# Transposing the softmax weights by 32 x 32 squares and DMA in place of TensorE, in a fused attention and experts kernel

## The chip, the cores and the metric

The kernel runs on one core of a Trainium2 chip. The metric is the device time of one execution in microseconds (us), as a median over runs. The core has five engines, each of which runs its own instructions in order: TensorE (PE in the profile, with PEld for its weight loads), VectorE (DVE), ScalarE (ACT), GpSimd (POOL) and SyncE (SP). Engines wait for each other through semaphores. SP and ACT issue plain DMAs, GpSimd issues indirect ones, and sixteen DMA engines carry the packets of all of them.

## What is computed

Eight images of 256 channels and 32 x 32 places go through two layers, all in float32. Layer 0 is an attention with eight heads, whose softmax runs over the queries. Layer 1 takes the 1024 places of an image as tokens `t` of 256 numbers:

```python
t = t + _L1_attn_ref(_ln_t(t), L1_attn_W)
t = t + _L1_ffn_ref(_ln_t(t), router_w, w1, b1, w2, b2)   # 8 experts, best 2 of each token

def _L1_attn_ref(x, W):
    xa = jnp.einsum('bnd,ed->bne', x, W)
    scores = jnp.einsum('bne,bme->bnm', xa, x)
    attn = jax.nn.softmax(scores, axis=-1)
    return jnp.einsum('bnm,bmd->bnd', attn, x)
```

The change lies in the last line: the product of the 1024 x 1024 weights `attn` with the normed tokens.

## The kernel before

The kernel is written in a tile language: a scheduler orders each engine's instructions and sets the semaphores, and tiles with the same tag share a fixed number of buffers. Images are handled one after the other. For each image `b` the kernel runs `layer0`, then `attend` (the first line above), then the routing of the tokens to experts. For images 0 to 6 the routed tokens are scattered to DRAM, and the experts run once for all seven after layer 0 of image 7. Image 7 runs `attend` while results of the other seven are collected, and then its experts densely.

`attend` treats the 1024 tokens in eight blocks of 128 (`NT` = 8, `P` = 128). It norms the tokens into `n1`, turns them to channels (`nT`), and multiplies by `W` (`xa`). Then, for block `i`:

- `scores(i)`: four matmuls (L670) write the block's 128 x 1024 scores to PSUM (`ps1`, one of three buffers of the tag "big"). VectorE takes the maximum of each row (L678). ScalarE writes the exponentials `ex` to SBUF and their sums `ssum` (L681). `ex` is in a pool of six buffers with the tag "exps", each 128 x 1024.
- `mix(i)`: a matmul that sums over the tokens `m` needs `m` on the partitions, and `ex` has them along its rows. So TensorE transposes eight 128 x 128 pieces against an identity (L689), VectorE copies the 128 x 1024 result from PSUM to `aT` in SBUF (L691), and eight matmuls with `aT` as the stationary side add up `py` (L695). VectorE scales by the reciprocal of `ssum` and adds the tokens (L699, L701).

The loop at L706 issues `mix` one block behind `scores`. TensorE's order that comes of it is: the transposes of block i, half of the scores of block i + 2, the products of block i, the other half of those scores. While VectorE and ScalarE work, TensorE also does products of the next image (`fill`, `pv` and `pqk`, L387 and L328). SP loads the next image (`xT`, L93) and its 32 x 32 squares (`xs`, L427, eight DMAs of 128 KB in runs of 512 bytes).

Two operations elsewhere in the kernel resemble what the change adds. The stores of the results (L1186, L1193) transpose a 128 x 1024 tile on VectorE by 32 x 32 squares and send it off in DMAs of 256 runs of 512 bytes; the last four of them are issued by ACT. `b_v` (L118) is loaded in 1024 runs of 256 bytes.

The functions before the change, with the profile's line numbers:

Of the kernel before, what the change touches and what calls it, by code (L numbers as in the profile page):

```python
# [10 lines left out]
F32 = mybir.dt.float32  # L11
# [8 lines left out]
def kernel(  # L20
# [23 lines left out]
    nc = tc.nc  # L44
    P = 128
    B, C, S = x.shape
    E, D, FF = w1.shape
# [4 lines left out]
    NT = S // P  # L52
# [15 lines left out]
    expp = ctx.enter_context(tc.tile_pool(name="expp", bufs=6))  # L68
# [6 lines left out]
    def big(name):  # L75

        return ps_big.tile([P, 1024], F32, tag="big", name=name)

    def acc(name):

        return ps_acc.tile([P, 512], F32, tag="acc", name=name)
# [54 lines left out]
    for e in range(E):  # L136
# [30 lines left out]
        fill=0.0,  # L167
# [42 lines left out]
    SQ = 32  # L210
    NQ = P // SQ
# [40 lines left out]
    def layer_norm(t, dst, eps, name):  # L252
        return Norm(t, dst, eps, name).blocks(0, NT)

    def to_channels(t, dst, name):

        for cc in range(NCC):
            pt = big(f"pt_{name}_{cc}")
            for i in range(NT):
                nc.tensor.transpose(pt[:, ts(i, P)], t[:, i, ts(cc, P)], ident)  # L260
            copied = nc.vector.tensor_copy(dst[:, cc, :], pt)
        return copied
# [380 lines left out]
    def attend(b, t1, fill, tick=nothing):  # L643
        n1 = one.tile([P, NT, D], F32, tag="n", name=f"n1_{b}")
        layer_norm(t1, n1, 1e-5, f"a{b}")
        fill("norm 1")
        nT = one.tile([P, NCC, S], F32, tag="nT", name=f"nT_{b}")
        to_channels(n1, nT, f"n1_{b}")
        fill("normed 1")
        xa = one.tile([P, NCC, S], F32, tag="xa", name=f"xa_{b}")  # L650
        for ec in range(NCC):
            px = big(f"px_{b}_{ec}")
            for dc in range(NCC):
                for n in range(NH2):
                    nc.tensor.matmul(  # L655
                        px[:, ts(n, 512)],
                        WT[:, dc, ts(ec, P)],
                        nT[:, dc, ts(n, 512)],
                        start=(dc == 0),
                        stop=(dc == NCC - 1),  # L660
                    )
            tick(("xa", ec), nc.vector.tensor_copy(xa[:, ec, :], px))

        t2 = t1

        def scores(i):
            psc = big(f"ps1_{b}_{i}")
            for ec in range(NCC):
                for n in range(NH2):
                    nc.tensor.matmul(  # L670
                        psc[:, ts(n, 512)],
                        xa[:, ec, ts(i, P)],
                        nT[:, ec, ts(n, 512)],
                        start=(ec == 0),
                        stop=(ec == NCC - 1),
                    )
            nmax = small.tile([P, 1], F32, tag="nmax", name=f"nmax_{b}_{i}")
            tick(("max", i), nc.vector.tensor_reduce(nmax, psc, AX.X, ALU.max, negate=True))  # L678
            ex = expp.tile([P, 1024], F32, tag="exps", name=f"ex1_{b}_{i}")
            ssum = small.tile([P, 1], F32, tag="ssum", name=f"ssum_{b}_{i}")  # L680
            nc.scalar.activation(ex, psc, AF.Exp, bias=nmax, scale=1.0, accum_out=ssum)  # L681
            return ex, ssum

        def mix(i, ex, ssum):
            if i == NT - 1:
                fill("last weights")
            pt = big(f"pa_{b}_{i}")
            for m in range(NT):
                nc.tensor.transpose(pt[:, ts(m, P)], ex[:, ts(m, P)], ident)  # L689
            aT = two.tile([P, S], F32, tag="tr", name=f"aT_{b}_{i}")  # L690
            nc.vector.tensor_copy(aT, pt)  # L691
            ahead = fill("last products") if i == NT - 1 else None
            py = acc(f"py_{b}_{i}")
            for m in range(NT):
                nc.tensor.matmul(  # L695
                    py[:, :D], aT[:, ts(m, P)], n1[:, m, :], start=(m == 0), stop=(m == NT - 1)
                )
            rs = small.tile([P, 1], F32, tag="rs1", name=f"rs1_{b}_{i}")
            nc.vector.reciprocal(rs, ssum)  # L699
            with tc.issue_after(ahead.ins) if ahead else nullcontext():  # L700
                mixed = nc.vector.scalar_tensor_tensor(  # L701
                    t2[:, i, :], py[:, :D], rs, t1[:, i, :], ALU.mult, ALU.add
                )
            tick(("mixed", i), mixed)

        pending = None  # L706
        for i in range(NT):
            now = (i, *scores(i))
            if pending is not None:
                mix(*pending)  # L710
            pending = now
        mix(*pending)
        return t2


# [87 lines left out]
    def normed(b, t2, fill, tick=nothing, norm=None):  # L803

        if norm is None:
            n2 = one.tile([P, NT, D], F32, tag="n", name=f"n2_{b}")
            tick("normed", layer_norm(t2, n2, 1e-5, f"f{b}"))
        else:
            n2 = norm.dst
            tick("normed", norm.blocks(NT - 1, NT))  # L810
        fill("norm 2")
        nT = one.tile([P, NCC, S], F32, tag="nT", name=f"n2T_{b}")
        tick("turned", to_channels(n2, nT, f"n2_{b}"))

        nc.gpsimd.tensor_add(t2, t2, n2)  # L815
        fill("normed 2")
        l = logits(b, nT)
        return n2, nT, l
# [256 lines left out]
    class Results:  # L1075
# [94 lines left out]
        def tick(self, place, behind=None):  # L1170
            added, sent, stored = self.PLACES.get(place, (0, 0, 0))
            if added:
                with tc.issue_after(behind.ins):
                    for _ in range(added):
                        self.add()
            for _ in range(sent):
                self.gather(behind)
            for _ in range(stored):
                if self.whole:
                    b, total, n = self.whole.pop(0)  # L1180
                    store(b, total, n)
# [130 lines left out]
    for b in range(B):  # L1312
        xT = next_x
        if b + 1 < B:
            next_x = load_x(b + 1)
        if b > 0:
            xs = load_squares(b)
        t1 = layer0(b, xT, begun, routing, xs)
        if b + 1 < B:
            begun = Begin(b + 1, next_x)  # L1320
            t2 = attend(b, t1, begun.at)
            n2, _, l = normed(b, t2, begun.at)
            nc.sync.dma_start(groups[0].sums[b], t2)
            routing = dispatch(b, n2, l, groups[0])
            continue
        experts(groups[0])
        others = Results(groups[0])
        others.begin()
        norm = None

        def fill(place):

            nonlocal norm
            others.tick(place)
            if place == "last products":
                norm = Norm(t1, one.tile([P, NT, D], F32, tag="xa", name=f"n2_{b}"), 1e-5, f"f{b}")
                return norm.blocks(0, NT - 1)

        t2 = attend(b, t1, fill, others.tick)
        dense(b, t2, norm, others.tick)  # L1340
        assert others.added == len(others.units) and not others.whole
# [42 lines left out]
```

## Time and profile before

| | us |
|---|---|
| median of 3 runs | 2407.27 |
| lowest and highest | 2404.34 to 2408.37 |
| profiled execution, its own time | 2406.31 |
| its span, first to last instruction | 2404.6 |
| TensorE busy in it | 2359.7 |
| VectorE busy | 1540.9 |
| ScalarE busy | 938.0 |
| `attend` of the second image, scores(0) to the last product | 66.95 |

The profile is one execution of the program. In a group of instructions the last column says how long the engine had been idle before them and who ended that; the column before it gives the total busy time and the mean duration of one. The chain of waits is followed back from the last instruction to what released it each time; what lies on it sets the time.

### The profile page before, as it was taken

The numbers are of one execution on the slowest core, as the hardware profiler recorded it, in microseconds if no ns is written. First come the engines' busy times: TensorE is split into PE (matmuls) and PEld (weight loads), VectorE is DVE, ScalarE is ACT, GpSimd is POOL, SyncE is SP. The second block draws the span as 40 slices with busy tenths as digits, with TensorE's granted clock in tenths as the row PEclk, the third lists the DMA queues.
The fourth block names the chain that finished last, engine by engine and source line by source line (L and its number), as shares of the span: only waits on it lengthen the run. The fifth ranks groups of instructions, "written<-read, shape, count | busy, mean of one in ns | idle before, by whom it ended". The sixth has DMA issues, their size and how long they took to land.

```text
span 2404.6 us, 36813 instructions
## 1 busy us (share of the span) xinstructions
PE 2359.7 (98%) x13759; PEld 1316.5 (55%) x13759; DVE 1540.9 (64%) x3660; ACT 938.0 (39%) x1570; POOL 420.0 (17%) x391
## 2 busy tenths in 40 slices
PE   9999999999999999999999999999999999999898
PEld 3356534654466336633664356435653388887565
DVE  5775587457845785578647864687468753334776
ACT  3651366126611662156315641465136622221111
POOL 0000012000200020003000200020002234444563
PEclk9999999999999999999999999999999999999899
DMA  8993201010101010001000100100010256665454
GB/s 294 386 386 101 53 19 36 1 36 12 43 1 35 8 47 1 18 18 54 1 18 18 47 8 6 31 25 12 1 36 19 74 176 220 219 219 161 142 170 119
DMA packets 114778, 196.59 MB, mean 82 GB/s; under 512 B 15752, under 2 KB 58408, under 8 KB 112808
## 3 DMA queue, kind: packets, MB, share of 16 engines
q1 hardware_dynamic: 88504, 126.52, 15.8%
q0 software_dynamic: 25008, 67.20, 9.1%
q8 instruction: 109, 1.79, 0.3%
q10 hardware_dynamic: 1088, 0.52, 0.1%
q14 instruction: 69, 0.57, 0.1%
HBM read 108.88 MB, written 110.90 MB: 91 GB/s over the span
## 4 chain that ended last, share of the span: by engine, by line
PE 91%; DVE 5%; ACT 2%; DMA 1%; issue 1%; POOL 0%; SPq 0%; DVEq 0%; ACTq 0%; POOLq 0%
PE po L545 19%; PE psc L468 18%; PE py L695 9%; PE ps L670 7%; PE pqk L350 7%; PE pr L636 5%; PE ph L1021 4%; PE pv L387 4%; PE pe L1046 4%; PE pdh L1250 2%; PE px L655 2%; PE pdy L1274 2%; PE pa L689 2%; PE pqk L328 2%; PE px L1011 1%
## 5 line engine op out<-in xcount | busy, mean ns | idle before, releaser
L509 ACT ACTIVATE ex<-psc,nmax 128x1024 f32<-128x1024 f32 x512 | 570.5, 1115 | 312.6 <-DVE scrap L492 227.8
L468 PE MATMUL psc<-qk,qk 64*64 64x512 f32 x4096 | 578.4, 594 | 10.3 <-ACT ex L509 10.3
L545 PE MATMUL po<-ex,vs 64*64 64x512 f32 x4096 | 573.5, 592 | 1.3 <-DVE vs L525 0.3
L492 DVE TENSOR_SCALAR_CACHE_REDUCE scrap<-psc,nmax 128x512 f32<-128x512 f32 x512 | 384.4, 751 | 152.0 <-PE psc L468 126.2
L483 DVE TENSOR_REDUCE nmax<-psc 128x1 f32<-128x512 f32 x512 | 350.3, 684 | 9.3 <-PE psc L468 9.3
L468 PEld LDWEIGHTS psc<-qk,qk 64*64 64x64 f32 x4096 | 181.0, 132 | 285.8 <-ACT ex L509 138.0
L545 PEld LDWEIGHTS po<-ex,vs 64*64 64x64 f32 x4096 | 177.9, 132 | 273.5 <-issue 81.7
L695 PE MATMUL py<-n,aT 128*128 128x256 f32 x1024 | 238.0, 386 | 2.9 <-DVE aT L691 2.9
L670 PE MATMUL ps<-nT,xa 128*128 128x512 f32 x512 | 236.0, 592 | 0.0
L695 PEld LDWEIGHTS py<-n,aT 128*128 128x128 f32 x1024 | 191.7, 191 | 66.6 <-DVE aT L691 41.8
L884 POOL DMA_INDIRECT rows<-n,d_at x112 | 108.8, 972 | 662.6 <-DVE nmax L483 662.3
L681 ACT ACTIVATE ex<-ps,nmax 128x1024 f32<-128x1024 f32 x64 | 71.3, 1115 | 348.0 <-DVE nmax L678 333.5
L815 POOL TENSOR_TENSOR t<-t,n 128x2048 f32<-128x2048 f32 x8 | 36.3, 4534 | 924.0 <-DVE n L242 924.0
L350 PE MATMUL pqk<-xT,wqkv 128*128 128x512 f32 x384 | 171.2, 599 | 0.0
L701 DVE SCALAR_TENSOR_TENSOR t<-py,rs,t 128x256 f32<-128x256 f32 x64 | 30.9, 482 | 194.4 <-PE py L695 194.4
L670 PEld LDWEIGHTS ps<-nT,xa 128*128 128x128 f32 x512 | 93.5, 190 | 81.2 <-issue 75.1
L350 PEld LDWEIGHTS pqk<-xT,wqkv 128*128 128x128 f32 x384 | 71.0, 190 | 99.9 <-issue 77.8
L1130 POOL DMA_INDIRECT yk<-y,yat x112 | 110.6, 988 | 72.4 <-issue 26.8
L636 PEld LDWEIGHTS pr<-wo,res 128*128 128x128 f32 x512 | 120.7, 331 | 3.7 <-ACT res L563 3.7
L636 PE MATMUL pr<-wo,res 128*128 128x256 f32 x512 | 121.6, 398 | 0.3 <-ACT res L563 0.3
L387 PE MATMUL pv<-wqkv,xT 128*128 128x512 f32 x256 | 120.3, 599 | 1.4 <-DVE v L395 1.0
L315 ACT ACTIVATE qk<-pqk,b_qks 128x512 f32<-128x512 f32 x124 | 85.6, 691 | 88.9 <-PE pqk L350 79.8
(189 smaller groups left out, 2479.8 us busy)
## 6 DMA issues: line engine op xcount, KB each, us to landing
rows<-wb SPq DMA_DIRECT2D x7, 8192.0 KB, 51.7
y<-yb SPq DMA_DIRECT2D x63, 256.0 KB, 2.4
xs<-in_x_dram SPq DMA_DIRECT2D x64, 128.0 KB, 3.9
out_dram<-oT SPq DMA_DIRECT2D x60, 128.0 KB, 2.9
xT<-in_x_dram SPq DMA_DIRECT2D x7, 1024.0 KB, 5.0
sums<-t SPq DMA_DIRECT2D x7, 1024.0 KB, 3.9
o<-sums SPq DMA_DIRECT2D x7, 1024.0 KB
wpack<-in_L_ffn_w_dram SPq DMA_DIRECT2D x4, 1024.0 KB
```

The costliest lines, as they stand in the source:

```text
L350: mm = nc.tensor.matmul(pq[:, ts(n, 512)], wqkv[:, cc, t, ts(g, P)], xT[:, cc, ts(n, 512)], start=(cc == 0), stop=(cc == NCC - 1),)
L387: nc.tensor.matmul(pv, self.xT[:, cc, ts(i, P)], wqkv[:, cc, 2, :], start=(cc == 0), stop=(cc == NCC - 1),)
L468: mm = nc.tensor.matmul(pss[at, h][ts(c, DK), ts(n, 512)], k[r, j * P + c * DK : j * P + (c + 1) * DK], q[r, ts(n, 512)], start=True, stop ...
L483: firsts[at, h] = nc.vector.tensor_reduce(nmax, pss[at, h][:, ts(0, 512)], AX.X, ALU.max, negate=True)
L492: seconds[h] = nc.vector.tensor_scalar(scrap, pss[at, h][:, ts(1, 512)], -1.0, nmaxes[at, h], ALU.mult, ALU.min, accum_out=nmax,)
L509: nc.scalar.activation(ex, pss.pop((at, h)), AF.Exp, bias=nmaxes.pop((at, h)), scale=1.0, accum_out=sums[at][:, h : h + 1],)
L545: mm = nc.tensor.matmul(po[n][ts(h, DK), :], vss[at][keys, h, :], exps[at, h][keys, ts(n, 512)], start=(j == 0 and turn == 0), stop=(j == ...
L636: nc.tensor.matmul(pr[:, :C], own(res[:, g, :], i), wo[:, g, :], start=(g == 0), stop=(g == NPAIR - 1))
L670: nc.tensor.matmul(psc[:, ts(n, 512)], xa[:, ec, ts(i, P)], nT[:, ec, ts(n, 512)], start=(ec == 0), stop=(ec == NCC - 1),)
L695: nc.tensor.matmul(py[:, :D], aT[:, ts(m, P)], n1[:, m, :], start=(m == 0), stop=(m == NT - 1))
L884: scatter = nc.gpsimd.indirect_dma_start(out=view[:, :], out_offset=bass.IndirectOffsetOnAxis(ap=ats[k][:, i : i + 1], axis=0), in_=n2[:, ...
L1130: ins = nc.gpsimd.indirect_dma_start(out=self.slot(at)[:, k, :], out_offset=None, in_=self.group.y[:, :], in_offset=bass.IndirectOffsetOnAxis(
```

## The change

For blocks 0 to 6 the weights are no longer transposed on TensorE. VectorE transposes each 32 x 32 square of `ex` in place (`sq`). Sixteen DMAs, eight from SP and eight from ACT, then move the squares to where they belong in a dense `aT`: DMA (a, k) reads the 32 partitions of group a and writes the 32 partitions of group k, in 256 runs of 32 numbers (128 bytes), 32 KB in all. `sq` and `aT` are taken from the six "exps" buffers. Block 7 is turned as before. `mix` now runs two blocks behind the scores in the program's text instead of one, and the last two turned blocks and block 7 are mixed after the loop.

```diff
-        def mix(i, ex, ssum):
-            if i == NT - 1:
-                fill("last weights")
+        def turn(i, ex):
+            sq = expp.tile([P, S], F32, tag="exps", name=f"sq_{b}_{i}")
+            nc.vector.transpose(sq, ex)
+            aT = expp.tile([P, S], F32, tag="exps", name=f"aT_{b}_{i}")
+            to = aT.rearrange("p (m a q) -> p a m q", a=NQ, q=SQ)
+            since = sq.rearrange("p (m k q) -> p k m q", k=NQ, q=SQ)
+            for a in range(NQ):
+                queue = (nc.sync, nc.scalar)[a % 2]
+                for k in range(NQ):
+                    queue.dma_start(to[ts(k, SQ), a], since[ts(a, SQ), k])
+            return [aT[:, ts(m, P)] for m in range(NT)]
+
+        def turn_last(i, ex):
             pt = big(f"pa_{b}_{i}")
             for m in range(NT):
                 nc.tensor.transpose(pt[:, ts(m, P)], ex[:, ts(m, P)], ident)
             aT = two.tile([P, S], F32, tag="tr", name=f"aT_{b}_{i}")
             nc.vector.tensor_copy(aT, pt)
+            return [aT[:, ts(m, P)] for m in range(NT)]
+
+        def mix(i, aT, ssum):
             ahead = fill("last products") if i == NT - 1 else None
             py = acc(f"py_{b}_{i}")
             for m in range(NT):
                 nc.tensor.matmul(
-                    py[:, :D], aT[:, ts(m, P)], n1[:, m, :], start=(m == 0), stop=(m == NT - 1)
+                    py[:, :D], aT[m], n1[:, m, :], start=(m == 0), stop=(m == NT - 1)
                 )
...
-        pending = None
+        pending = []
         for i in range(NT):
-            now = (i, *scores(i))
-            if pending is not None:
-                mix(*pending)
-            pending = now
-        mix(*pending)
+            ex, ssum = scores(i)
+            if i < NT - 1:
+                pending.append((i, turn(i, ex), ssum))
+            if i > 1:
+                mix(*pending.pop(0))
+        fill("last weights")
+        pending.append((NT - 1, turn_last(NT - 1, ex), ssum))
+        for some in pending:
+            mix(*some)
```

Here `SQ` is 32 and `NQ` is 4. In the changed file the transpose on VectorE stands at L688, the DMAs at L695, the products at L711 and the update at L717.

## The prediction

> **What bounds the kernel now.** I read the page first: busy shares and the chain that ended last.
>
> ```profile
> PE 2359.7 (98%) x13759; PEld 1316.5 (55%) x13759; DVE 1540.9 (64%) x3660; ACT 938.0 (39%) x1570; POOL 420.0 (17%) x391
> PE 91%; DVE 5%; ACT 2%; DMA 1%; issue 1%; POOL 0%; SPq 0%; DVEq 0%; ACTq 0%; POOLq 0%
> ```
>
> TensorE (PE) carries 91% of the chain, so work taken off it shortens the kernel wherever nothing else becomes late. Next the chain of waits in the second image's `attend` (449.31 to 516.26 us, 66.95 us), which holds all that the change touches:
>
> ```profile
> 449.31 3.45 PE ps L670 x8
> ...
> 456.64 1.09 PE pa L689 x8
> 457.73 1.72 PE ps L670 x4
> 459.45 3.45 PE py L695 x16
> 462.90 1.72 PE ps L670 x4
> 464.62 0.87 PE pa L689 x8
> 465.49 1.72 PE ps L670 x4
> 467.21 3.58 PE py L695 x16
> ```
>
> From 459.45 on there is no gap: a block costs 3.44 (scores) + 0.87 (transposes) + 3.57 (products) = 7.88 us of PE, two blocks 15.77. The head, scores(0) to py(0), is 10.14 us. Third, the groups of instructions by form (busy total, mean ns of one) give the prices off PE:
>
> ```profile
> L678 DVE TENSOR_REDUCE nmax<-ps 128x1 f32<-128x1024 f32 x64 | 78.1, 1220 | 58.6 <-PE ps L670 58.6
> L691 DVE COPY aT<-pa 128x1024 f32<-128x1024 f32 x64 | 77.9, 1217 | 1.8 <-PE pa L689 1.8
> L681 ACT ACTIVATE ex<-ps,nmax 128x1024 f32<-128x1024 f32 x64 | 71.3, 1115 | 348.0 <-DVE nmax L678 333.5
> L1186 DVE STREAM_TRANSPOSE oT<-o 128x1024 f32<-128x1024 f32 x14 | 28.5, 2034 | 0.1
> ```
>
> Fourth, DMA prices. Two stretches of the DMA view (9.4 to 11.4 us, where the 256-byte runs of `b_v` pass, and 754.1 to 759.9, the 512-byte runs of `xs`), the issues, and SP's timeline:
>
> ```profile
> DMA packets 1209, 0.46 MB, mean 230 GB/s; under 512 B 1079, under 2 KB 1197, under 8 KB 1209
> q1 hardware_dynamic: 1209, 0.46, 90.0%
> ```
> ```profile
> q1 hardware_dynamic: 2176, 1.05, 97.1%
> ```
> ```profile
> out_dram<-oT ACTq DMA_DIRECT2D x4, 128.0 KB, 3.5
> ```
> ```profile
> 753.24 3.78 SPq L427 DMA_DIRECT2D xs<-in_x_dram  x8
> ```
>
> So a packet holds one of 16 engines for 0.90 x 16 x 2.0 / 1209 = 24 ns where most are 256 bytes, and 0.971 x 16 x 5.8 / 2176 = 41 ns at 512 bytes. A stretch of 0.7 us from 203.7 us on, mostly 8-byte runs, gives 0.964 x 16 x 0.7 / 635 = 17 ns. A DMA of 256 runs occupies its queue for 3.78 / 8 = 0.47 us.
>
> **What goes.** Blocks 0 to 6 of eight images lose the eight PE transposes and the PSUM copy: 56 x 0.87 = 48.7 us of PE, all on the chain, and 56 x 1.22 = 68.3 us of VectorE, off it. Nothing is saved at block 7, which keeps the old way.
>
> **What comes.** On VectorE 56 StreamTransposes at 2.03 us (L1186, same shape): +0.81 us a block against the copy. VectorE then holds reduce 1.22, transpose 2.03, reciprocal 0.16, update 0.48, statistics 0.61 = 4.5 us a block; it does not bound by its sum, only by its order. On SP and on ACT eight DMAs a block, 896 in all, each 256 runs of 128 bytes. No run of 128 bytes stands in the trace: 17 ns bounds a packet from below, 41 from above; I take 24, the 256-byte row being nearest in size. With its one 4-byte completion packet (9 ns, the median of the trace) beside 16 runs on each engine, a DMA costs the 16 engines (16 x 24 + 9) / 1000 = 0.39 us each, above the 0.235 at which two queues can issue. The 16 of a block take 16 x 0.39 = 6.3 us, plus 1.25 us from issue to first packet and 0.4 us from last packet to landing. These last two are an estimate: the ACT-issued store of 128 KB shared the engines with SP's and landed after 3.5 us; two such transfers of 17 packets at about 40 ns take 1.4, which leaves 2.1, cut to 1.65 as the bare first store on SP landed after 2.4. So D, first issue to last landing, is 7.9 us; 6.1 at 17 ns, 12.3 at 41.
>
> A rule to weigh: the Trainium skill ("DMA: Bandwidth & Descriptors", Specifications) says that transfers below 512 bytes are done as read-modify-write, so, as I read it, a short run should cost no less than a 512-byte one; by it D would be the 12.3 of the upper end. The 24 ns of the 256-byte stretch, against 41, speaks against that here, and I stay with the row.
>
> **What moves, and what queues behind it.** I read the order and waits of the built program. (1) ACT: exp(i+1) stands behind the eight DMA issues of block i, which wait for the VectorE transpose of block i. Eight completion counters serve both queues, four each, so the fifth issue of a queue waits for its first to land. (2) VectorE: transpose(i+2) stands behind the update t<-py(i) and reduce(i+4). (3) PE: order is scores 0 to 3, a quarter of scores 4, mix 0, the rest of scores 4, and so on; mix(i) waits for all 16 DMAs. (4) From block 3 on exp(i) also waits for mix(i-3), whose buffer it takes; mix(i-3) is long over by (1). (5) SP: the next image's `xs` loads now stand between the DMAs of blocks 4 to 6 and wait for scores 7; transpose(5) comes after reduce(7) anyway, so they cost nothing unless SP falls behind. No GpSimd work is passed.
>
> (2) and (3) close a loop over two blocks: mix(i) 3.57, three quarters of scores(i+4) 2.59, reduce 1.22, transpose 2.03, handoffs and waits about 0.5 (estimate: some ten, at the 0.02 to 0.05 the chain shows as "issue" and PE's drain), then D, then mix(i+2): 9.9 + D = 17.8 us, where it was 15.77. (1) closes another over one block: exp with its read-out 1.31, transpose 2.03, handoffs 0.3, and the issues until the last is out, about 1.25 + 8 x 0.39 + 0.4 + 0.47 = 5.2, together 8.9: the same pace. PE itself needs only 7.01 a block and now waits some 3.7 us in two blocks.
>
> An image then is: head 7.3 (scores 0 until exp 0 ends, 449.31 to 456.60), transpose 2.03 with handoffs 0.2, D 7.9 = 17.4; three loops to mix 6, 53.4; mixes 6 and 7, 7.15: 78.0 us against 66.95, +11.0. Eight images: +88 us.
>
> **The clock.** Two stretches of the windows view after pauses of PE (the columns are stretch, us, PE busy, PEld, DVE, ACT, POOL, clock, DMA share, GB/s):
>
> ```profile
> 1866.80:1873.50 6.70, 5.36 (x28) 1.72 (x32) 3.68 (x9) 3.61 (x6) 3.16 (x4) 0.50 0.84 257
> 2259.30:2262.60 3.30, 3.30 (x10) 2.57 (x9) 1.29 (x3) 0.00 (x0) 1.62 (x2) 0.50 1.01 415
> ```
>
> The first follows 6.0 us without a matmul, the second 2.6 us (2256.0 to 2258.6). The new loop's pauses are of 1 to 3 us. A fall to 0.50 for 3.4 us costs 1.7 us; none in a loop costs nothing, one in each of four loops 6.8 us an image. Half of that, 3 us, gives +24.
>
> The Trainium skill ("TensorE: Matmul & The Clock Gate", HAM oscillation) puts the idle gap that halves the clock at about 3.4 us; by it few of these pauses would count and the 24 would go. The fall after 2.6 us decides for keeping it.
>
> Sum: 88 + 24 = +112 us on the profiled execution's 2406.31 (span 2404.6 and 1.7 around it); the median of the runs, 2407.27, stands 1 us higher: 2519 us.
>
> **Rivals.** (a) Faster: the DMAs are hidden and PE's 48.7 us come out, 2358 us. An image breaks even where head, three loops and end (46.4 + 4D) equal 66.95, at D = 5.1 us: 13 ns a packet. Copies that stay inside SBUF, which the trace before does not show, might be that quick, but 8-byte packets cost 17 here, and the issues alone (8 x 0.47) with the latency make 5.4. To reach the full gain the issue queues would have to take far less than 0.47. Chance 0.05. (b) Much slower: 128-byte packets cost what 512-byte ones do, D = 12.3, 95.6 us an image, +229, and the clock falls in each loop, +54: 2690. For: both queues write the same 32 partitions at once. Against: the 24 ns row. Chance 0.17. (c) The edit changes nothing to be measured, because 17 ns packets make the loop 16.0 and the clock holds: 70.8 an image, +31 us, 2438; true no change needs D within 0.2 us of 5.1. That cheap-packet case has 0.13, no change 0.02. The forecast itself has 0.63.
>
> A difference under about 0.2% (5 us) can't be told from none. Faster 0.05, same 0.02, slower 0.93. The range reaches to the cheap-packet case below and into (b) above: 2436 to 2640.
>
> **What would show it.** In the profile after: L695 DMAs with D near 8 us and packets near 24 ns; PE waiting before L711 for DMA; exp L681 every 8.5 to 9 us instead of 7.88; StreamTranspose L688 x56 near 2.05; the PE clock below 1.00 in `attend`. If L711 follows L670 without gaps, the prediction is wrong, and D is under 5.

## The result, and the profile after

The changed kernel takes 2508.57 us (median of 4 runs, 2504.36 to 2511.07) against 2406.6 us of the kernel before, run beside it: a ratio of 1.0419, 95% interval 1.0403 to 1.0434. It is slower by 4.2%. The profiled execution took 2509.21 us, 102.9 more than the one before; its span is 2507.5. The busy line and the chain that ended last, of the changed kernel:

```profile
PE 2346.4 (94%) x13311; PEld 1289.1 (51%) x13311; DVE 1539.7 (61%) x3660; ACT 938.0 (37%) x1570; POOL 420.7 (17%) x391
PE 75%; DVE 6%; DMA 5%; ACTq 4%; issue 4%; SPq 3%; ACT 1%; DVEq 0%; POOLq 0%
```

PE lost 448 matmuls, the 56 x 8 transposes, but its idle time (span less busy) rose from 44.9 to 161.1 us. These 116 us of idle time are the price of the change. On the chain, PE's share fell from 91 to 75%, and the DMAs (DMA, ACTq, SPq) took 12%. The granted clock of the whole run fell from 0.994 to 0.978. Added up as half the length of each stretch at 0.50, TensorE lost 54 us to it, where it lost 15 before. The three parts (transposes, idle time, clock) agree with the whole: -48.7 + 116 + 39 = 106, against 102.9 (part of the slow clock fell into waits).

Where the time went by image, from the first matmul of the scores (L670) to the last product: before 67.1 us in each of seven images and 68.7 in the eighth; after 85.9, 78.3, 79.7, 77.7, 76.9, 77.2, 77.0 and 89.8. That is +104.2 us, all of the difference.

The groups that answer to those of before, by form:

```profile
L688 DVE STREAM_TRANSPOSE sq<-ex 128x1024 f32<-128x1024 f32 x56 | 69.4, 1239 | 39.1 <-ACT ex L681 39.1
L681 ACT ACTIVATE ex<-ps,nmax 128x1024 f32<-128x1024 f32 x64 | 71.3, 1114 | 444.2 <-DMA aT<-sq 401.5 <-DVE nmax L678 15.3 <-DVE t L717 13.8
L670 PE MATMUL ps<-nT,xa 128*128 128x512 f32 x512 | 236.1, 603 | 46.2 <-ACT ex L681 46.2
L711 PE MATMUL py<-n,aT 128*128 128x256 f32 x1024 | 250.4, 402 | 37.5 <-DMA aT<-sq 22.4 <-DMA xs<-in_x_dram 7.8 <-DMA out_dram<-oT 6.6
```

Two things are to be read here. The transpose took 1.24 us, no more than the copy that it replaces. And the long wait is `exp`'s: before, it waited 333.5 us for the maximum, the ordinary wait for work; now 401.5 of its 444.2 us end with the DMAs. PE waits for `exp` (the scores need the PSUM buffer that `exp` reads) more than for the DMAs themselves.

ScalarE's timeline in the second image shows the queue (columns: start, us, what; in brackets the idle time before):

```profile
480.34 1.11 ACT L681 ACTIVATE ex<-ps,nmax 128x1024 f32<-128x1024 f32 x1 [7.39 <-DMA aT<-sq]
481.35 0.19 ACT L681 ACTIVATION_READ_ACCUMULATOR ex<-ps,nmax 128x1 f32 x1
482.86 5.25 ACTq L695 DMA_DIRECT2D aT<-sq  x8
488.21 1.11 ACT L681 ACTIVATE ex<-ps,nmax 128x1024 f32<-128x1024 f32 x1 [6.66 <-DMA aT<-sq]
```

`exp` ends at 481.5, VectorE transposes until 482.8, eight issues run from 482.86 to 488.11, and the next `exp` starts 0.1 us after the last of them. The page names a DMA as what ended the wait, since landings fall at the same moment; the engine's own issues fill it. The price of an issue, and the packets of a stretch in which only these DMAs ran (475.5 to 480.5 us), stand in the view of the tile `aT` and in the DMA view:

```profile
L695 ACTq DMA_DIRECT2D aT<-sq x448: 592/624/1747, 207.1 to 2359.0; - x150
L695 SPq DMA_DIRECT2D aT<-sq x448: 585/611/1358, 220.9 to 2359.0; - x150
```
```profile
q10 hardware_dynamic: 1844, 0.22, 30.3%
q1 hardware_dynamic: 1632, 0.20, 26.6%
```

An issue holds its queue for 0.61 to 0.62 us (minimum, median and maximum in ns), and they follow each other every 0.66. A packet of 128 bytes took 0.303 x 16 x 5.0 / 1844 = 13 ns. The DMA engines were just over half busy: in this stretch they are not the bound, the queues are.

### The profile page after: what moved, and what is told of

Same layout as the page of the kernel before. It is cut to its first block, busy times and chain, and to the rows that moved or that the text cites. A ratio compares the mean times of both kernels' runs of the same rounds, so it can differ in the third digit from the quotient of the medians.

```text
span 2507.5 us, 37351 instructions
## 1 busy us (share of the span) xinstructions
PE 2346.4 (94%) x13311; PEld 1289.1 (51%) x13311; DVE 1539.7 (61%) x3660; ACT 938.0 (37%) x1570; POOL 420.7 (17%) x391
## 4 chain that ended last, share of the span: by engine, by line
PE 75%; DVE 6%; DMA 5%; ACTq 4%; issue 4%; SPq 3%; ACT 1%; DVEq 0%; POOLq 0%
PE po L545 18%; PE psc L468 18%; PE pqk L350 6%; PE pr L636 5%; ACTq L695 4%; PE py L711 4%; PE pv L387 4%; PE ph L1042 3%; SPq L695 3%; PE pe L1067 3%; DMA aT<-sq 3%; PE ps L670 3%; PE pdh L1271 2%; PE px L655 2%; PE pdy L1295 2%
## 5 line engine op out<-in xcount | busy, mean ns | idle before, releaser
L711 PE MATMUL py<-n,aT 128*128 128x256 f32 x1024 | 250.4, 402 | 37.5 <-DMA aT<-sq 22.4
L670 PE MATMUL ps<-nT,xa 128*128 128x512 f32 x512 | 236.1, 603 | 46.2 <-ACT ex L681 46.2
L711 PEld LDWEIGHTS py<-n,aT 128*128 128x128 f32 x1024 | 207.7, 204 | 97.7 <-issue 52.2
L681 ACT ACTIVATE ex<-ps,nmax 128x1024 f32<-128x1024 f32 x64 | 71.3, 1114 | 444.2 <-DMA aT<-sq 401.5
L670 PEld LDWEIGHTS ps<-nT,xa 128*128 128x128 f32 x512 | 95.8, 191 | 165.6 <-issue 90.8
L717 DVE SCALAR_TENSOR_TENSOR t<-py,rs,t 128x256 f32<-128x256 f32 x64 | 30.9, 482 | 198.6 <-PE py L711 198.6
L678 DVE TENSOR_REDUCE nmax<-ps 128x1 f32<-128x1024 f32 x64 | 78.3, 1224 | 101.4 <-PE ps L670 101.4
L387 PE MATMUL pv<-wqkv,xT 128*128 128x512 f32 x256 | 128.7, 630 | 11.4 <-ACT ex L681 9.7
L1151 POOL DMA_INDIRECT yk<-y,yat x112 | 111.3, 993 | 92.7 <-DVE t L717 29.9
L350 PEld LDWEIGHTS pqk<-xT,wqkv 128*128 128x128 f32 x384 | 71.0, 190 | 99.9 <-issue 76.8
```

What stands on the lines that cost most here:

```text
L350: mm = nc.tensor.matmul(pq[:, ts(n, 512)], wqkv[:, cc, t, ts(g, P)], xT[:, cc, ts(n, 512)], start=(cc == 0), stop=(cc == NCC - 1),)
L387: nc.tensor.matmul(pv, self.xT[:, cc, ts(i, P)], wqkv[:, cc, 2, :], start=(cc == 0), stop=(cc == NCC - 1),)
L670: nc.tensor.matmul(psc[:, ts(n, 512)], xa[:, ec, ts(i, P)], nT[:, ec, ts(n, 512)], start=(ec == 0), stop=(ec == NCC - 1),)
L711: nc.tensor.matmul(py[:, :D], aT[m], n1[:, m, :], start=(m == 0), stop=(m == NT - 1))
L1151: ins = nc.gpsimd.indirect_dma_start(out=self.slot(at)[:, k, :], out_offset=None, in_=self.group.y[:, :], in_offset=bass.IndirectOffsetOnAxis(
```

## The experiments

The theory T: ScalarE's in-order queue sets the pace, because `exp(i+1)` stands behind the eight issues of block i. The rivals: R1, the transfers themselves (packets, DMA engines); R2, the new order, with the products two blocks behind; R3, whatever is saved returns elsewhere. Every run is compared with runs of the kernel before on the same chip: 2423.75 us for e1 to e4, 2423.0 for e5 to e7, 2406.47 for e8.

**e1: ScalarE's issues one `exp` later** (edit shortened)**.**

```diff
-            for a in range(NQ):
+            def send(part):
+                for a in range(part, NQ, 2): ...      # the same DMAs, SP's or ScalarE's half
+            send(0); later.append(send)
...
             ex, ssum = scores(i)
+            if later:
+                with tc.issue_after(exped[-1].ins):   # behind exp(i) on ScalarE
+                    later.pop()(1)
```

> All DMAs of the turn stay; ScalarE's eight of block i are put behind exp(i+1) in ScalarE's order. Theory (T): in the changed kernel the pace of 8.5 us a block is set on ScalarE's in-order queue, exp 1.2 + wait for the transpose 1.3 + eight issues at 0.66 + the last landing, because exp(i+1) stands behind the eight issues of block i. By T the queue then needs 1.2 + 8 x 0.66 = 6.5 us a block, TensorE's 7.0 us bound, an image's attend falls from 78 to 59-64 us and the time to 2355-2400 us. Rival R1 (the transfers themselves, packets and 16 DMA engines, set the pace): same bytes, same engines, 2490-2515. Rival R2 (mixing two blocks behind, with the order of VectorE and PSUM buffers, sets the pace): 2490-2515.

Measured: 2443.36 us, ratio 1.0073 (1.0051 to 1.0095). The same DMAs, bytes and issues now cost 0.7% and not 4.2%, so R1 falls; but T's 2355 to 2400 was missed. Two stretches of its second image show both (columns: stretch, us, busy PE, PEld, DVE, ACT, POOL, clock, DMA share, GB/s):

```profile
480.00:490.00 10.00, 10.00 (x36) 6.47 (x35) 5.48 (x8) 1.21 (x2) 0.00 (x0) 1.00 0.54 81
500.00:510.00 10.00, 6.65 (x27) 5.41 (x27) 3.42 (x9) 2.33 (x4) 0.00 (x0) 0.87 0.55 83
```

In the loop PE is full: scores 3.44 and products 3.57, 7.0 us a block, as T says. At the end of `attend` it isn't. `exp` comes every 6.0 to 7.8 us, where T had 6.5, so ScalarE's queue falls behind. PE waits 1.4 us for the DMAs of block 4 (until 501.44) and 2.0 us for `exp(7)`, which starts at 505.83, behind ScalarE's half of block 5. ScalarE's half of block 6 stands behind `exp(7)` in turn: its last issue starts at 513.86, and the products of block 6 at 517.45. PE's clock is 0.50 for 3.4 us. Image 1 takes 76.8 us against e3's 66.4: SP's DMAs of its first block come only at 211.84, behind eight weight loads. Images 2 to 7 take 66.4 to 67.6 us against e3's 66.4; the six microseconds saved in the loop are lost at its end.

One thing besides the queue changed: the scheduler now lets the scores run further ahead. PE does 42 matmuls of scores, five and a quarter blocks, before the products of block 0:

```profile
456.89 18.19 PE L670 MATMUL ps<-nT,xa 128*128 128x512 f32 x42
474.92 3.62 PE L718 MATMUL py<-n,aT 128*128 128x256 f32 x16
```

In the changed kernel it does 34 there (four and a quarter blocks). The scores run as far ahead as in e1 in all later runs with DMAs except e4. So e1 does not test the queue at an order that is otherwise the same, and R2 is left to e3 and e4.

**e2: all sixteen on SP.**

```diff
-                queue = (nc.sync, nc.scalar)[a % 2]
+                queue = nc.sync
```

> All sixteen DMAs of a block are issued by SP, none by ScalarE. T: exp is free, but one queue issues 16 x 0.66 = 10.6 us a block, so the pace becomes 10.6 to 11 us instead of 8.5 and the time 2600-2660 us. R1 (transfers set the pace; bytes and engines unchanged): 2490-2530. A third outcome, only the blocking of exp matters: below 2480.

Measured: 2648.52 us (one run), as T said. The line of its tile view reads `x896` with the same median:

```profile
L695 SPq DMA_DIRECT2D aT<-sq x896: 3/609/1977, 211.4 to 2485.8; - x180
```

SP's issues follow each other without a break in its chain, sixteen every 10.5 us, and an image takes 95.5 to 100 us. The bytes and the engines are those of the changed kernel; only the number of issues in a row has doubled.

**e3: the new order with the old turn.**

```diff
-                pending.append((i, turn(i, ex), ssum))
+            pending.append((i, ex, ssum))
             if i > 1:
-                mix(*pending.pop(0))
+                j, ex, ssum = pending.pop(0)
+                mix(j, turn_last(j, ex), ssum)
...
```

> The old turn for every block (eight PE transposes, PSUM copy, no DMA) but the new order: mix two blocks behind the scores. T: the order itself costs little, TensorE still has 7.88 us a block, 2400-2425 us. R2 (the order costs): most of the 102 us stays, 2470 or more.

Measured: 2424.23 us, ratio 0.9999 (0.9989 to 1.0008). Being two blocks behind costs nothing by itself.

**e4: the same runs in twice as many DMAs.**

```diff
-                    queue.dma_start(to[ts(k, SQ), a], since[ts(a, SQ), k])
+                    for h in range(2):
+                        queue.dma_start(to[ts(k, SQ), a, ts(h, 4)], since[ts(a, SQ), k, ts(h, 4)])
```

> Each DMA is cut in two of 128 runs of 128 bytes: 32 issues a block, the same runs and bytes. If an issue costs by its runs (0.62 us for 256, then 0.31 for 128) T expects 2505-2530 us. If an issue costs a fixed 0.6 us, T expects 16 x 0.66 = 10.6 us of issues on ScalarE a block, 5.3 more, 56 blocks: about 2800 us. R1: 2510-2530 either way, as the packets are the same but for 16 more completions a block.

Measured: 2805.29 us (one run), at the mark of the fixed price:

```profile
L696 ACTq DMA_DIRECT2D aT<-sq x896: 592/612/1279, 207.1 to 2640.9; - x180
```

A DMA of 128 runs holds its queue as long as one of 256 did, 0.61 us. Between these two the cost goes by the number of DMAs, not by runs or bytes. This run also has the changed kernel's order (34 matmuls of scores ahead of the first products), so it tells T from R2. ScalarE's loop is then `exp` 1.3, transpose 1.25, sixteen issues 10.6 and waits of 0.2 to 0.5, 13.5 us a block. The loop by the order, mix(i) to mix(i+2), is at about 10.5: 8.7 us of products, scores, maximum and transpose, and some 12 us of transfers, for two blocks. In the second image `exp` came every 13.0 to 13.8 us. The order sets no such pace; R2 is out.

**e5 and e6: e1 in the first five or six blocks of images 2 to 8.** The rest goes by TensorE.

```diff
+        TURNED = 5 if b else 0            # e6: 6
...
+            pending.append((i, turn(i, ex) if i < TURNED else ex, ssum))
```

> As e1 (ScalarE's eight issues of block i behind exp(i+1)), but only blocks 0 to 4 of images 2 to 8 go by DMA; blocks 5 to 7, and all of image 1, go by TensorE and the PSUM copy. In e1's image 2 TensorE ran without a gap from 457 to 499 us and then waited for block 6's DMAs (gaps of 1.4 and 2.0 us, and a clock of 0.50 for 3.4 us), and image 1 waited behind weight loads on SP. T: those waits go, 35 blocks keep the saving of 0.87 us, 30 us: 0.985-0.993 of the time before. R3 (what was saved comes back elsewhere, at the end of attend or as a lower clock, whichever blocks go by DMA): 1.00-1.01.

> As e5, with blocks 0 to 5 by DMA. T: 42 blocks x 0.87 = 36 us if block 5's DMAs land in time, 0.983-0.990; if block 5 is late as block 6 was in e1, worse than e5, 0.995-1.005.

Measured: e5 2405.6 us, 0.9923 (0.9909 to 0.9936), inside T's range; e6 2418.93, 0.9975 (0.9963 to 0.9988), the second of its branches. Images 2 to 7 of e5 take 63.1 to 63.8 us, so 2.6 to 3.3 of the 4.35 us (5 x 0.87) stay. In e6 they take 63.6 to 65.9, no better although one block more is saved: PE now pauses up to 1.6 us in them. The profiled execution of e6 (2412.4 us, near the low end of its runs, 2410.35 to 2421.75) is 6.5 us longer than that of e5, and images 2 to 7 are together 6.7 us longer. Image 8's `attend` is longer too, 86.2 us against 78.6, but what follows it is shorter by more: from its start to the end of the program e6 takes 226.0 us and e5 227.3.

**e7: GpSimd in ScalarE's place, all blocks and images.**

```diff
-                queue = (nc.sync, nc.scalar)[a % 2]
+                queue = (nc.sync, nc.gpsimd)[a % 2]
```

> The changed kernel with ScalarE's eight DMAs of a block issued by GpSimd. T: exp no longer stands behind issues; if a GpSimd issue takes what its indirect ones take in the profile (0.97 us), eight take 7.8 us a block, pace about 8 us, 2460-2510; if it takes 0.6-0.7 us, about e1's 2420-2450. R1 (transfers): as the changed kernel, 2500-2530.

Measured: 2408.43 us in one run, below both of T's ranges and 14.6 below the kernel before on the same chip (2423.0); the changed kernel's time was 100 us longer, on another chip. GpSimd can issue such plain DMAs as well as indirect ones; the kernel before has three of them (`W_rows`, `r_rows`, `b_rows`). GpSimd's issue and the third image's `attend`, and below it that of e3:

```profile
L695 POOL DMA_DIRECT2D aT<-sq x448: 582/584/658, 207.7 to 2245.7; - x150
```
```profile
693.00:753.40 60.40, 60.40 (x212) 39.28 (x211) 29.07 (x48) 10.92 (x17) 32.26 (x56) 1.00 0.52 79
```
```profile
696.80:763.20 66.40, 66.40 (x266) 44.29 (x265) 29.96 (x48) 12.20 (x18) 0.00 (x0) 1.00 0.09 16
```

PE is busy for all of the 60.4 us at a clock of 1.00; e3 takes 66.4. That is the full 6.1 us (7 x 0.87) less 0.1. The order of scores is that of e1, five and a quarter blocks ahead. ScalarE issues nothing, so neither `exp(7)` nor block 6's DMAs wait for it. Image 8 is the exception (a stretch of it):

```profile
2220.00:2240.00 20.00, 11.45 (x34) 9.15 (x35) 8.37 (x16) 2.49 (x3) 16.65 (x22) 0.68 0.63 148
```

There GpSimd gathers the experts' results (L1151, 0.95 us each) and SP stores outputs in between the DMAs. It is GpSimd's queue that is late: SP's half of each block starts 2.2 to 20.7 us before GpSimd's, which stands between gathers, and from block 3 on the products start 1.7 to 2.2 us after the end of GpSimd's. For block 4, SP's half starts at 2202.38, GpSimd's runs as below, and the products start at 2223.30:

```profile
2215.93 0.95 POOL L1151 DMA_INDIRECT yk<-y,yat  x1 [0.30 <-issue]
2216.89 4.71 POOL L695 DMA_DIRECT2D aT<-sq  x8
```

Image 8's `attend` takes 90.3 us; e3's takes 76.0 on another chip. From image 8's start to the end of the program e7 takes 239.0 us and e3 230.2. Image 1 takes 68.6 against 66.4.

**e8: e7 in images 2 to 7 only.**

```diff
+        TURNED = range(NT - 1 if 0 < b < B - 1 else 0)
...
+            pending.append((i, turn(i, ex) if i in TURNED else ex, ssum))
```

> As e7 (SP and GpSimd issue, ScalarE none), but by DMA only in images 2 to 7; image 1, where weight loads stand ahead on SP, and image 8, where the last groups' gathers and loads run on GpSimd and SP, keep TensorE's transposes throughout. In e7 images 2 to 7 took 60.4 us of attend against 66.4 in e3, and images 1 and 8 took 68.6 and 90.3 against 66.4 and 76.0. T: the six images keep 6.0 us each, 36 us, and the other two lose nothing: 0.983-0.988 of the time before, 2380-2394 us if before is 2423. R3 (most comes back outside attend: e7's images follow each other every 243.7 us against 248.5): 6 x 4.8 = 29 us, 0.987-0.990.

Measured: 2372.58 us against 2406.47, ratio 0.9859 (0.9843 to 0.9875): 33.9 us faster than the kernel before, where T said 36 and R3 29.

```profile
PE 2325.9 (98%) x13423; PEld 1282.8 (54%) x13423; DVE 1533.3 (65%) x3660; ACT 937.3 (40%) x1570; POOL 615.6 (26%) x727
```

The span is 2370.4, so PE idles for 44.5 us, as before the change (44.9), and most of the 336 transposes less (42 x 0.87 = 36.5 us) comes out as time. T and R3 are each right in part. Images 2 to 7 take 60.4 to 60.5 us, as T said, and images 1 and 8 lose nothing (66.4 and 65.7 us, against 67.1 and 68.7 before). But images 2 to 7 follow each other every 243.6 us, 4.9 less than in e3, so 1.1 of the 6.0 us saved in `attend` comes back outside it, as R3 said. Against the kernel before it is 5.5 us less, 33 us in six images, as the new order alone has an `attend` of 66.4 us where it was 67.1.

The chip counts in such comparisons: image 8 is the same code in e3 and e8, and from its start to the end of the program e3 took 230.2 us on its chip and e8 203.9 on another. The change itself was sound; the queue that issued half of it was not.

## Why the prediction was right, and where it was not

The time was forecast at 2519 and came at 2509 (2508.57 median), for the reason given: the loop through ScalarE's issues, which delay `exp`. Several of its terms were wrong all the same, and that the time came out so close is partly luck. By its steps:

- **What goes** held. 448 matmuls left PE, and where nothing else became late (e7, e8) 6.0 of the 6.1 us an image came out of `attend`.
- **VectorE's transposes** were mis-sized: 2.03 us a piece were taken from L1186, 1.24 were measured. That row reads the same shape, but writes and reads permuted views; in the changed kernel it still takes 2.03 (now L1207) beside the 1.24 of L688.
- **D** was 7.9 us; in block 1 of the second image it was about 6.9 (first issue 482.86, last at 487.78, landing 2.0 later). Two of its terms were wrong in opposite directions. A packet was priced at 24 ns, from the 256-byte row; it took 13. The row was misread: that stretch holds 1040 packets of 256 bytes at a mean of 18 ns, and 118 of 1 KB and 12 of 6 KB that raise the average. In the same way the 8-byte packets of the stretch at 203.7 us took 9 ns and not 17, so 17 was no lower bound. An issue was priced at 0.47 us, from 512-byte loads; it took 0.62, spaced 0.66. So the prediction thought the DMA engines slower than the queues (0.39 us a DMA against 0.235), and it is the other way round: 16 x 13 + 9 = 217 ns a DMA against 0.33 for two queues. Rival (a)'s break-even of 13 ns a packet was met to the nanosecond, and it did not help, since the issues alone made D 6.9. (The rival's own objection, that issues and latency make 5.4, was right in kind and short by 1.5.) With 18 ns the prediction's own sum has a D of 6.4 and a time of 2472 us; the misread row brought it nearer to the result.
- **The rule on transfers under 512 bytes** (the Trainium skill, "DMA: Bandwidth & Descriptors", Specifications) would have made D 12.3. Here 128-byte packets between SBUF partitions took 13 ns against 41 in the 512-byte stretch from DRAM of the kernel before, so short runs were not dearer. No run shows the price that it would set.
- **The loops.** Two were put at the same pace, 8.9 us a block. ScalarE's is the real one: `exp` 1.3, transpose 1.25, issues 5.25 to 6.0 (6.8 in block 6), handoffs and waits up to 0.8. From mix 0 (482.56) to mix 4 (516.07) it took 8.4 us a block, and in this image each `exp` starts 0.05 to 0.2 us after the last issue before it. The prediction's 5.2 us for these issues was met by luck: it was made of packets (8 x 0.39), latency and the fifth issue's wait for the first landing. The runs show eight issues at 0.66 instead; in block 1 the first DMA landed at 484.89, before the fifth was issued at 485.49. The two-block loop, by its measured terms (products 3.5, scores 2.8, maximum 1.2, transpose 1.2, D 6.9), is about 15.6 us, 7.8 a block: slower than PE's 7.0, but not the bound. e4, at the same order, ran at ScalarE's pace. In e1 and e7 the pace fell to PE's 7.0, with ScalarE's queue cut and the scores a block further ahead, which eases the two-block loop too; how much of the 1.4 us each of the two is worth was not separated. e3 shows that being two blocks behind is free.
- **An image** was put at 78.0 us without the clock and the second took 78.2 with it. The head was 16.9 (17.4 said), the loops half a microsecond a block shorter, and the end longer: PE's order has block 7's transposes ahead of mix 6, and they wait for `exp(7)`, which stands behind block 6's issues (it starts at 531.54). The prediction let mixes 6 and 7 follow at once.
- **The clock** was put at +24 us and measured at about +39. In images 2 to 7 the halved stretches cost 20 us, 3.4 an image where 3 was said. The rest is in images 1 and 8.
- **Images 1 and 8** were treated as the others. They lost 18.8 and 21.1 us, the others 10.7 on average. In image 1 SP's weight loads (to 220.8 us) stand ahead of its turn DMAs, which begin 13.8 us after ScalarE's; step (5) named only the `xs` loads as strangers on SP. In image 8 SP is not late: its DMAs start within 0.01 us of ScalarE's. There VectorE also adds up the experts' results (L1173) and transposes them for the stores (L1207), so that the transposes of the weights start up to 3.8 us after their `exp` (11.5 us in seven blocks, 1.6 in image 5), and ScalarE's eight issues take up to 6.7 us (43.6 against 38.1), while GpSimd's gathers use the DMA engines as well.

In block 2 of image 8, whose `exp` ended at 2307.0, this looks as follows:

```profile
2305.64 3.25 DVE L1173 SCALAR_TENSOR_TENSOR o<-yk,gate,o 128x256 f32<-128x256 f32 x8
2309.94 1.24 DVE L688 STREAM_TRANSPOSE sq<-ex 128x1024 f32<-128x1024 f32 x1
2311.21 6.71 ACTq L695 DMA_DIRECT2D aT<-sq  x8
```

Images 2 to 7 were put at 14 us each (11 and the clock's 3) and lost 10.7, 20 us less in all; images 1 and 8 were put at 28 together and lost 40, 12 more. Most of the one error cancels the other: the total is better than its parts. Of the signs that the prediction named, three came: PE waiting before L711 for DMAs, `exp` every 7.9 to 8.7 us up to block 6 and 9.3 at block 7 in the second image (8.5 to 9 was said), and a clock below 1.00, as in the row below. Three did not: D near 8 us, packets near 24 ns, and transposes near 2.05 us. The row is of the changed kernel's second image:

```profile
525.00:535.00 10.00, 7.17 (x25) 5.79 (x24) 1.45 (x5) 2.49 (x3) 0.00 (x0) 0.69 0.52 95
```

Left open: why an issue of these DMAs costs 0.62 us (not the wait for a landing, as shown above), and how the gain of e1 and e7 divides between ScalarE's queue and the order of the scores. That permuted views make a VectorE transpose slower is read from two lines, not tried.

## What to carry to other kernels

Count the DMAs that a step issues and put them on a queue by that count times the price of an issue, before asking about bytes: sixteen small DMAs a block were cheap for the DMA engines and dear for the two engines that issued them. An engine that computes on the path should not issue them ahead of its own next instruction; the same work on an idle engine's queue turned +4.2% into -0.6% (e7, one run). And look at each queue in each repetition of the loop: the first and last image had other work on the same queues, and leaving the change out there was worth 10 us by the profiles of e7 and e3, or 19 by the times of e7 and e8 (each against the kernel before on its own chip), of a gain of 34.

## What the runs showed of the hardware

- An SBUF-to-SBUF DMA between 32 partitions held an SP or ScalarE queue for 0.61 us with 128 runs and with 256; loads of 256 runs of 512 bytes from DRAM had held it 0.47.
- GpSimd, expected at 0.97 us an issue from its indirect DMAs, issued these in 0.58, quicker than SP in the same run (0.61). Its queue recorded 14,336 packets for 448 DMAs, in each 16 of 2 KB and 16 of 4 bytes, where SP's recorded packets of 128 bytes.
- In the changed kernel the clock was halved after pauses of PE from 2.1 us on, but not after all: seven pauses of 2.19 to 2.25 us and one of 2.99 had no fall behind them, and none of 1.9 us or less had. In e1 it also fell after pauses of 1.96 and 1.56 us, so these runs give no sharp limit. The idle gap of about 3.4 us that the Trainium skill gives ("TensorE: Matmul & The Clock Gate", HAM oscillation) is longer than ten of the changed kernel's pauses that brought a fall, for example 2.83 us at 530.0.
